# Three of seven row blocks of a depthwise convolution on TensorE, in the last pair of images

## The chip, the cores and the metric

The kernel runs on one core of one Trainium2 chip. The metric is the device time of one launch in microseconds. Below, VectorE, ScalarE, GpSimd (POOL) and TensorE (PE) are the four compute engines; SyncE (SP) issues most of the transfers. All data are fp32.

## What is computed

The reference has two layers over 32 images of 64 channels and 56 x 56 pixels. The first adds sums of products of two and of three channels of a group to its input. The second is an attention over the pixels with two softmaxes, and this change lies in what follows it:

```python
out = jnp.einsum('nabcd,nicd->niab', f, g)
out = out / h * w
out = jax.lax.conv_general_dilated(out, w_dw, (1, 1), ((1, 1), (1, 1)),
        dimension_numbers=('NCHW', 'OIHW', 'NCHW'), feature_group_count=n_in)
out = _bn(out, gamma2, beta2, mean2, var2)
return out + l
```

`feature_group_count=n_in` makes it a depthwise convolution: each channel has its own 3 x 3 filter, with one pixel of zeros around the image. `l` is the input of the second layer. The batch norm is a factor and an offset per channel; the kernel folds the factor into the nine weights (`wdt`, line 299) and keeps the offset as `bias2`.

## The kernel before

The images are worked in 16 pairs (`NP`), with 2 x 64 channels on the 128 partitions. A pair has 49 tiles of 128 query pixels (`IT`), and the main loop (line 889) takes one tile an iteration: two halves of scores on TensorE, negated and reduced by VectorE, two exponentials on ScalarE, and three iterations later (`LAG`) the product with the values, summed in PSUM over all tiles of an image. Work of the neighbouring pairs is put beside it. `put` (line 679) gives each piece a place, an iteration and a slot in it ("loads", "feed", "gap0", "gap1"); `pin` (line 89) then fixes the order of every engine to the order in which the program was written out. So each engine and each queue runs its list front to back.

After the last tile of an image, `take` divides the sums (`num`), `turn` transposes them (`tr`), and `place` (line 632) writes them by eight transfers an image into `tt`, a tile of 128 channels by 3136 pixels that all pairs share. The transfers go by halves of the image: pixels 0 to 1599 first (`j` = 0), the rest after.

The convolution reads `tt` and adds into `ys[n % 3]`, a tile in SBUF that holds `l`, one of three that rotate. The rows of the image are in five blocks (`NB`, `BLK`, line 309), of 11 rows, the last of 12. For each block, `conv_begin` (line 651) lets POOL add `bias2`; nine calls of `conv_step` (line 655) let VectorE add one tap each, `y = tt shifted * weight + y`, without the row or column that would lie outside the image; then `store` (line 671) starts the transfer to the output. The 45 steps of a pair are spread over the next pair's iterations (line 869 on). For the last pair nothing follows, and its steps come one after another behind the last tile.

The tiles that the change uses: `xs`, a tag of the pool `xp` with 13 buffers (line 315), holds loaded inputs of the first layer's products, the last of which belong to the last pair and are read by POOL one pair earlier; `ps`, four banks of PSUM, holds the scores.

Of the kernel before, what the change touches and what calls it, by code (L numbers as in the profile page):

```python
# [9 lines left out]
FP = mybir.dt.float32  # L10
AF = mybir.ActivationFunctionType
ALU = mybir.AluOpType
# [6 lines left out]
H = W = 56  # L19
# [3 lines left out]
HALF = NCH // 2  # L23
# [3 lines left out]
BANK = 512  # L27
# [8 lines left out]
PCH = -(-N // NPC)  # L36
# [33 lines left out]
def tile_poly_conv_attention(  # L70
# [12 lines left out]
    NP = B // 2  # L83
    IT = 2 * NQ + 1
# [29 lines left out]
    pe, dve, act, pool, sync = map(Pinned, (nc.tensor, nc.vector, nc.scalar, nc.gpsimd, nc.sync))  # L114

    const = ctx.enter_context(tc.tile_pool(name="const", bufs=1))
    xp = ctx.enter_context(tc.tile_pool(name="xp", bufs=2))
# [6 lines left out]
    ps = ctx.enter_context(tc.tile_pool(name="ps", bufs=1, space=PSUM))  # L124
# [7 lines left out]
    at = 0  # L132
    for s, (_, bs) in enumerate(STEPS):
        for h in range(2) if s < NSLOT else ():
            act.dma_start(
                out=wq[s::NSLOT, :, h, :],
                in_=wpoly[h * 32 : h * 32 + 32, at : at + NRND, h * 32 : h * 32 + 32],
# [5 lines left out]
    wdt = const.tile([128, 9], FP, name="wdt")  # L143
# [12 lines left out]
    for k in range(2):  # L156
        pe.matmul(
            out=ax[:, k * 256 : k * 256 + 256],
            lhsT=w4,
            rhs=wq.rearrange("p k h o -> p (k h o)")[:, :256],  # L160
            start=(k == 0),
            stop=True,
            skip_group_check=True,
        )
    dve.memset(ax, 0.0)
    tt = const.tile([128, N], FP, name="tt")
# [31 lines left out]
    ys = [yt[:, p, :] for p in range(3)]  # L198
# [68 lines left out]
    for k in range(NRND):  # L267
        by = row("beta2_0") if k == 0 else b3row
        w = wq[:, k, :, :].rearrange("p h o -> p (h o)")
        dve.tensor_tensor(w, w, by, ALU.mult)  # L270
    for half in (0, C):
        w = w4[:, half : half + C]
# [4 lines left out]
    t0 = const.tile([128, 1], FP, name="t0")  # L277
# [22 lines left out]
    bias2 = const.tile([128, 1], FP, name="bias2")  # L300
# [5 lines left out]

    prods = {}
    NB = 5
    BLK = [(b * H // NB, (b + 1) * H // NB) for b in range(NB)]
    stored = set()  # L310


# [2 lines left out]
    XB = {"x0": 7, "xs": 13, "xc": 3}  # L315
# [6 lines left out]
    def start(out, in_):  # L322
        credit[0] -= 1
        sync.dma_start(out=out, in_=in_)
# [193 lines left out]
    def tile_at(t):  # L518
        n, r = divmod(t, IT)
        return n, (0 if r < NQ else 2 if r == NQ else 1), r % (NQ + 1)  # L520
# [128 lines left out]
    TAPS = [(4, 1, 1)] + [(k, *divmod(k, 3)) for k in range(9) if k != 4]  # L649

    def conv_begin(n, b):
        blk = ys[n % 3][:, BLK[b][0] * W : BLK[b][1] * W]
        pool.tensor_scalar(blk, blk, bias2, None, ALU.add)

    def conv_step(n, i):
        b, i = divmod(i, 9)
        k, dy, dx = TAPS[i]
        r0, r1 = max(BLK[b][0], 1 - dy), min(BLK[b][1], H + 1 - dy)
        x0, x1 = max(0, 1 - dx), min(W, W + 1 - dx)
        yr = ys[n % 3].rearrange("p (r w) -> p r w", w=W)[:, r0:r1, x0:x1]  # L660
        tr = tt.rearrange("p (r w) -> p r w", w=W)
        dve.scalar_tensor_tensor(
            yr,
            tr[:, r0 + dy - 1 : r1 + dy - 1, x0 + dx - 1 : x1 + dx - 1],
            wdt[:, k : k + 1],
            yr,
            ALU.mult,
            ALU.add,
        )

    def store(n, b):
        stored.add((n, b))
        blk = slice(BLK[b][0] * W, BLK[b][1] * W)
        start(out[2 * n : 2 * n + 2].rearrange("b c n -> (b c) n")[:, blk], ys[n % 3][:, blk])


# [2 lines left out]
    def put(t, at, what):  # L679
        beside.setdefault((t, at), []).append(what)  # L680
# [5 lines left out]
    LAG = 3  # L686
# [54 lines left out]
    def ready(qs):  # L741

        end = min(N, (qs[-1] + 1) * QT)
        return next(c for c, (p, w) in enumerate(PCS) if p + w >= end)
# [59 lines left out]
    for n in range(NP):  # L804
        base = n * IT
# [7 lines left out]
        if n == 0:  # L813
# [3 lines left out]
            for c in range(NPC):  # L817
                todo += rounds(1, c, ALL, 2)
                if c >= NPC // 2 + 1:
                    k = min(2 if c < NPC - 1 else len(ga), sum(ready(g[2]) <= c for g in ga))  # L820
# [3 lines left out]
            at = [2 * base + free[i * (len(free) - 1) // (len(todo) - 1)] for i in range(len(todo))]  # L824
        elif n + 1 == NP:
            todo = gb
            at = [2 * (base + LAG) + 3 + 4 * i for i in range(len(gb))]
        else:
            at = []
# [30 lines left out]
        for b, end in ((2 * n, base + NQ), (2 * n + 1, base + IT - 1)):  # L860
            t = end + LAG
# [7 lines left out]
    for n in range(NP):  # L869
        t0 = n * IT + IT + LAG + 5  # L870
        more = range(2 * t0, 2 * ((n + 2) * IT - 1))
        if n + 1 < NP:
            more = [h for h in more if h // 2 != (n + 1) * IT + NQ + LAG]
            more = [h for h in more if h not in leaves] if len(more) - len(leaves & set(more)) >= 9 * NB else more
        for i in range(9 * NB):
            at = more[i * (len(more) - 1) // (9 * NB - 1)] if n + 1 < NP else 2 * t0 + i
            put(at // 2, f"gap{at % 2}", lambda n=n, i=i: conv_step(n, i))
            if i % 9 == 0:
                put(at // 2 - 2, "gap0", lambda n=n, b=i // 9: conv_begin(n, b))
            if i % 9 == 8:  # L880
                put(at // 2 + 1, "loads", lambda n=n, b=i // 9: store(n, b))
# [6 lines left out]
    t = 0  # L888
    while t < last + LAG or beside:
# [3 lines left out]
        if old:  # L893
            n, kind, q = tile_at(u)
# [111 lines left out]
```

## Time and profile before

| | us |
|---|---|
| three runs | 4959.59, 4962.83, 4973.32 |
| median of the runs | 4962.83 |
| the profiled execution | 4963.24 |
| its span, first to last instruction | 4961.4 |

| engine | busy, us | share of the span | instructions |
|---|---|---|---|
| PE, matmuls | 4711.5 | 95% | 118068 |
| ScalarE | 4554.6 | 92% | 2356 |
| VectorE | 4136.2 | 83% | 6106 |
| PE, weight loads | 3211.9 | 65% | 118068 |
| POOL | 3212.2 | 65% | 4325 |

The profile records one execution. Its page gives the busy time of each engine, the chain of waits that ended last, and groups of like instructions with their mean duration and with what ended the idle time before them. Its timeline gives start and length of instructions, its windows the busy time of each engine in a stretch, with the clock that TensorE was granted (PEclk, 1.00 is full speed). An average over the span says little about a single stage: the shares above are those of the steady loop, while the change lies in the last tens of microseconds and in preparations before them. All instructions of the main function carry the line of the helper that records them (108), so groups are told apart by the names of their tiles: `y<-tt,wdt,y` is a step of the convolution, `tt<-tr` a transfer of `place`, `out_dram<-y` a store.

### The profile page before, as it was taken

The page shows a single profiled execution, that of the slowest core. Times are in us where ns is not written, and L with a number is a line of the kernel's source. Part 1 is how long each engine was busy: PE and PEld are TensorE (multiplying, and loading weights), DVE is VectorE, ACT ScalarE, POOL GpSimd, SP SyncE. Part 2 cuts the span into 40 slices and gives each one's busy share as a digit, 9 for nine tenths or more (in the row PEclk, how much of TensorE's full clock was granted, in tenths as well). Part 3 has the DMA queues.
Part 4 walks back from the last instruction along what each step waited for, and adds up shares of the span by engine and source line. Part 5 has one row for each costly group of instructions (what it writes and reads, how often), then busy time and mean ns, then how long its engine had stood idle before and what let it go on. Part 6 is the DMA issues. An engine that isn't in the chain of part 4 may idle for free.

```text
span 4961.4 us, 263901 instructions
## 1 busy us (share of the span) xinstructions
PE 4711.5 (95%) x118068; PEld 3211.9 (65%) x118068; DVE 4136.2 (83%) x6106; ACT 4554.6 (92%) x2356; POOL 3212.2 (65%) x4325
## 2 busy tenths in 40 slices
PE   6988999999999999999999999999999999999885
PEld 2555666666666666666666666666666666666663
DVE  6545898988888898898988888888888888888787
ACT  1767999999999999999999999999999999999995
POOL 2676685857758586785857678585876858587000
PEclk9999999999999999999999999999999999999997
DMA  7555656565565556556565555656555565654101
GB/s 203 148 154 150 147 143 154 144 149 143 146 148 147 139 150 149 139 143 150 146 146 148 147 142 144 145 152 145 144 150 144 145 145 146 153 142 117 39 8 33
DMA packets 884029, 685.64 MB, mean 138 GB/s; under 512 B 290892, under 2 KB 868428, under 8 KB 878796
## 3 DMA queue, kind: packets, MB, share of 16 engines
q1 hardware_dynamic: 874892, 659.46, 52.1%
q8 instruction: 923, 15.12, 1.3%
q10 hardware_dynamic: 8000, 9.30, 0.6%
q14 instruction: 214, 1.75, 0.1%
HBM read 565.65 MB, written 25.69 MB: 119 GB/s over the span
## 4 chain that ended last, share of the span: by engine, by line
PE 76%; DVE 12%; DMA 3%; issue 3%; ACT 3%; POOL 1%; SPq 1%; ACTq 0%; POOLq 0%; DVEq 0%
PE av L108 33%; PE ps L108 25%; PE ax L108 18%; DVE e L108 10%; ACT e L108 3%; DMA xc_None<-in_x_dram 2%; DVE y L108 1%; SPq L108 1%; POOL p L108 1%; DVE num L108 1%; DMA x<-in_x_dram 1%; DMA first<-in_x_dram 1%; POOL q L108 0%; DMA xa<-in_x_dram 0%; ACTq L108 0%
## 5 line engine op out<-in xcount | busy, mean ns | idle before, releaser
L108 PEld LDWEIGHTS av<-gq,e 128*64 128x64 f32 x64512 | 2015.8, 138 | 945.6 <-issue 938.6
L108 ACT ACTIVATE e<-e,nm 128x3136 f32<-128x3136 f32 x784 | 2283.6, 2913 | 279.9 <-DVE e L108 264.0
L108 POOL TENSOR_TENSOR p<-q,x 128x242 f32<-128x242 f32 (+1 forms) x2418 | 1820.2, 786 | 842.6 <-PE ax L108 834.8
L108 ACT ACTIVATE e<-e,rz 128x3136 f32<-128x3136 f32 x784 | 2270.5, 2896 | 0.0
L108 PE MATMUL av<-gq,e 128*64 128x65 f32 x64512 | 2229.3, 225 | 4.3 <-ACT e L108 3.0
L108 DVE TENSOR_SCALAR_CACHE_REDUCE e<-ps 128x1568 f32<-128x1568 f32 x784 | 1403.4, 1790 | 312.7 <-PE ps L108 295.4
L108 DVE TENSOR_SCALAR_CACHE_REDUCE e<-ps,nm 128x1568 f32<-128x1568 f32 x784 | 1448.3, 1847 | 256.9 <-PE ps L108 251.4
L108 PE MATMUL ps<-th 32*64 32x392 f32 x25088 | 1450.2, 515 | 120.6 <-DVE e L108 110.8
L108 DVE SCALAR_TENSOR_TENSOR y<-tt,wdt,y 128x605 f32<-128x605 f32 (+4 forms) x720 | 726.2, 1009 | 6.7 <-DMA tt<-tr 5.2
L108 POOL TENSOR_TENSOR p<-q,xb 128x242 f32<-128x242 f32 x806 | 574.9, 740 | 218.8 <-PE ax L108 208.5
L108 POOL TENSOR_TENSOR q<-x,xa 128x242 f32<-128x242 f32 x806 | 570.9, 732 | 204.9 <-DMA xa<-in_x_dram 195.5
L108 PEld LDWEIGHTS ps<-th 32*64 32x64 f32 x25088 | 369.9, 130 | 463.1 <-DVE e L108 381.6
L108 PE MATMUL ax<-gq,e 128*64 128x65 f32 x12288 | 490.3, 222 | 1.2 <-issue 1.2
L108 PE MATMUL ax<-p,wq 128*32 128x242 f32 (+1 forms) x6448 | 477.8, 374 | 2.4 <-POOL p L108 1.4
L108 PEld LDWEIGHTS ax<-gq,e 128*64 128x64 f32 x12288 | 425.4, 138 | 1.5 <-issue 1.5
L108 PEld LDWEIGHTS ax<-p,wq 128*32 128x32 f32 x6448 | 178.4, 109 | 108.4 <-POOL p L108 15.7
L108 POOL TENSOR_SCALAR y<-y,bias 128x616 f32<-128x616 f32 (+1 forms) x80 | 149.1, 1864 | 149.2 <-PE ax L108 149.2
L108 DVE SCALAR_TENSOR_TENSOR y<-ax,bias,xc_None 128x242 f32<-128x242 f32 (+3 forms) x208 | 97.1, 467 | 120.7 <-PE ax L108 115.1
L108 POOL TENSOR_TENSOR p<-xc_None 128x242 f32<-128x242 f32 (+3 forms) x208 | 127.6, 614 | 105.2 <-DMA xc_None<-in_x_dram 85.3
L108 PE MATMUL ax<-p,w 128*32 128x242 f32 (+1 forms) x1612 | 125.1, 373 | 33.2 <-POOL p L108 33.2
L108 PE MATMUL ax<-wit,y 128*64 128x64 f32 x3136 | 143.8, 223 | 10.2 <-issue 6.1
L108 ACT ACTIVATION_READ_ACCUMULATOR e<-e,nm 128x1 f32 x784 | 145.7, 186 | 0.0
(80 smaller groups left out, 1348.9 us busy)
## 6 DMA issues: line engine op xcount, KB each, us to landing
x<-in_x_dram SPq DMA_DIRECT2D x2232, 121.0 KB
xa<-in_x_dram SPq DMA_DIRECT2D x744, 121.0 KB
xb<-in_x_dram SPq DMA_DIRECT2D x1488, 60.5 KB
th<-y SPq DMA_DIRECT2D x124, 392.0 KB
xc_None<-in_x_dram SPq DMA_DIRECT2D x360, 121.0 KB
x<-in_x_dram SPq DMA_DIRECT2D x186, 116.0 KB
out_dram<-y SPq DMA_DIRECT2D x64, 308.0 KB
tt<-tr SPq DMA_DIRECT2D x128, 100.0 KB
```

The lines of the kernel that those rows point to most:

```text
L108: i = f(*args, **kw)
```

## The change

Only the last pair (`n` = 15) is touched; `BLK` gets a list of blocks per pair, which is the old one for the first 15. The last pair has seven blocks of 8 rows. VectorE computes blocks 0 to 3 (rows 0 to 31, `NDVE` = 4) by nine steps each, as before. TensorE computes blocks 4 to 6 (rows 32 to 55): a depthwise tap is a product with a diagonal matrix of the tap's 128 weights, and nine such matmuls with shifted columns of `tt` are summed in one bank of PSUM a block. VectorE then adds this sum, `bias2` and `y` in one instruction a block, behind its own four blocks; POOL adds no bias to these three.

The nine diagonal matrices are made by POOL from an identity, in ten of the `xs` buffers, at the fourth iteration after the start of the last pair ("feed", iteration 739). All 27 matmuls are written out ahead of VectorE's 36 steps. Blocks 0 to 3 are stored after their steps and blocks 4 to 6 after their additions, so that the last pair has seven stores for five. In the lists of the engines, POOL's eleven new instructions stand ahead of the biases of the last pair but one.

```diff
-    BLK = [(b * H // NB, (b + 1) * H // NB) for b in range(NB)]
+    BLK = [[(b * H // NB, (b + 1) * H // NB) for b in range(NB)]] * (NP - 1)
+
+    BLK.append([(r, r + 8) for r in range(0, H, 8)])
+    NDVE = 4
...
+    def make_diags():
+
+        eye = xp.tile([128, PCH], FP, name="eye", tag="xs", bufs=XB["xs"])[:, :128]
+        pool.memset(eye, 0.0)
+        pool.affine_select(
+            out=eye, in_=eye, compare_op=ALU.not_equal, fill=1.0, base=0, pattern=[[-1, 128]],
+            channel_multiplier=1,
+        )
+        for k in range(9):
+            t = xp.tile([128, PCH], FP, name=f"diag_{k}", tag="xs", bufs=XB["xs"])[:, :128]
+            pool.tensor_scalar(t, eye, wdt[:, k : k + 1], None, ALU.mult)
+            diags.append(t)
+
+    def conv_matmuls(n, blocks):
+        acc = ps.tile([128, HALF, BANK], FP, name="conv", tag="ps")
+        tr = tt.rearrange("p (r w) -> p r w", w=W)
+        for j, b in enumerate(blocks):
+            for i in range(9):
+                k, dy, dx, r0, r1, x0, x1 = tap(n, b, i)
+                rb = BLK[n][b][0]
+                o = acc[:, j, : 8 * W].rearrange("p (r w) -> p r w", w=W)
+                pe.matmul(
+                    out=o[:, r0 - rb : r1 - rb, x0:x1],
+                    lhsT=diags[k],
+                    rhs=tr[:, r0 + dy - 1 : r1 + dy - 1, x0 + dx - 1 : x1 + dx - 1],
+                    start=(i == 0),
+                    stop=(i == 8),
+                    skip_group_check=True,
+                )
+        return {b: acc[:, j, : 8 * W] for j, b in enumerate(blocks)}
+
+    def conv_end(n):
+
+        blocks = range(NDVE, len(BLK[n]))
+        accs = conv_matmuls(n, blocks)
+        for b in range(NDVE):
+            for i in range(9):
+                conv_step(n, 9 * b + i)
+            store(n, b)
+        for m in blocks:
+            y = ys[n % 3][:, BLK[n][m][0] * W : BLK[n][m][1] * W]
+            dve.scalar_tensor_tensor(y, accs[m], bias2, y, ALU.add, ALU.add)
+            store(n, m)
...
+        if n + 1 == NP:
+            put(n * IT + LAG + 1, "feed", make_diags)
+            for b in range(NDVE):
+                put(t0 - 4, "gap0", lambda n=n, b=b: conv_begin(n, b))
+            put(t0, "gap0", lambda n=n: conv_end(n))
+            break
         for i in range(9 * NB):
-            at = more[i * (len(more) - 1) // (9 * NB - 1)] if n + 1 < NP else 2 * t0 + i
+            at = more[i * (len(more) - 1) // (9 * NB - 1)]
```

`tap`, which the diff takes out of `conv_step`, gives the weight's number, the shift and the rows and columns that a tap reaches. `conv_begin`, `conv_step` and `store` index `BLK` by the pair.

More of the change, by code (lines that the diff above doesn't have):

```diff
@@ L651, in conv_begin, with tap @@
     def conv_begin(n, b):
-        blk = ys[n % 3][:, BLK[b][0] * W : BLK[b][1] * W]
+        blk = ys[n % 3][:, BLK[n][b][0] * W : BLK[n][b][1] * W]
         pool.tensor_scalar(blk, blk, bias2, None, ALU.add)
+    def tap(n, b, i):
+        k, dy, dx = TAPS[i]
+        r0, r1 = max(BLK[n][b][0], 1 - dy), min(BLK[n][b][1], H + 1 - dy)
+        x0, x1 = max(0, 1 - dx), min(W, W + 1 - dx)
+        return k, dy, dx, r0, r1, x0, x1
     def conv_step(n, i):
         b, i = divmod(i, 9)
-        k, dy, dx = TAPS[i]
-        r0, r1 = max(BLK[b][0], 1 - dy), min(BLK[b][1], H + 1 - dy)
-        x0, x1 = max(0, 1 - dx), min(W, W + 1 - dx)
+        k, dy, dx, r0, r1, x0, x1 = tap(n, b, i)
         yr = ys[n % 3].rearrange("p (r w) -> p r w", w=W)[:, r0:r1, x0:x1]
@@ L669, in conv_step @@
         )
+    diags = []
+    def make_diags():
[14 more added lines that the diff above has]
+            for i in range(9):
+                k, dy, dx, r0, r1, x0, x1 = tap(n, b, i)
+                rb = BLK[n][b][0]
[20 more added lines that the diff above has]
+            store(n, m)
     def store(n, b):
         stored.add((n, b))
-        blk = slice(BLK[b][0] * W, BLK[b][1] * W)
+        blk = slice(BLK[n][b][0] * W, BLK[n][b][1] * W)
         start(out[2 * n : 2 * n + 2].rearrange("b c n -> (b c) n")[:, blk], ys[n % 3][:, blk])
```

## The prediction

> **What bounds the kernel now.** The summary says that the kernel is bound by VectorE, ScalarE and TensorE in turn, but the change touches one stage only, so I went from the page to the last stretch. The timeline of the last 70 us comes first (start, length, engine, operation):
>
> ```profile
> 4909.54 0.64 PE L108 MATMUL ax<-gq,e 128*64 128x65 f32 x16
> ...
> 4911.57 1.90 DVE L108 STREAM_TRANSPOSE tr<-num 128x800 f32<-128x800 f32 x2
> 4918.71 39.58 DVE L108 SCALAR_TENSOR_TENSOR y<-tt,wdt,y 128x616 f32<-128x616 f32 x45 [5.23 <-DMA tt<-tr]
> 4926.55 32.13 SPq L108 DMA_DIRECT2D out_dram<-y  x5
> ```
>
> TensorE's last matmul ends at 4910.2. VectorE waits until 4918.71 for the transfers into `tt`, then runs the 45 steps of the last pair's convolution alone until 4958.29. The fifth store follows, and the span ends at 4961.4, 3.1 us later. The chain of waits agrees: from 4918.71 on it holds nothing but these steps. So this stage is VectorE's alone, and a microsecond taken from it is a microsecond of the span. The groups of the same stretch give durations (busy us, mean ns):
>
> ```profile
> L108 DVE SCALAR_TENSOR_TENSOR y<-tt,wdt,y 128x605 f32<-128x605 f32 x24 | 20.4, 848 | 0.9
> L108 DVE SCALAR_TENSOR_TENSOR y<-tt,wdt,y 128x616 f32<-128x616 f32 x12 | 10.3, 858 | 5.5 <-DMA tt<-tr 5.2
> ...
> L108 DVE SCALAR_TENSOR_TENSOR y<-tt,wdt,y 128x672 f32<-128x672 f32 x2 | 1.8, 915 | 0.0
> ```
>
> From 616 to 672 elements the time grows by 57 ns, 1.02 ns an element; I use 1.04, which also fits the 550-element row (792 ns). Over the stage the 45 steps cover 27,556 elements per partition ((56+55+55) rows by (56+55+55) columns, since edge taps lose a row or a column). 27,556 x 1.0417 ns = 28.70 us, and the rest of 39.58 us is 10.88 us, or 0.242 us a step.
>
> **VectorE's part of the change.** Four blocks of 8 rows keep 36 steps and (31+32+32) x 166 = 15,770 elements: 16.43 + 36 x 0.242 = 25.1 us. Removed are 9 steps and 11,786 elements: 12.28 + 2.18 = 14.45 us. Added are three additions that read PSUM, 448 wide. A row of the first stage is nearly the same instruction (PSUM, a column and an SBUF tile in, SBUF out), though on 64 partitions:
>
> ```profile
> L108 DVE SCALAR_TENSOR_TENSOR y<-first_s,bias,first 64x448 f32<-64x448 f32 x4 | 2.7, 671 | 1.9 <-PE first_s L108 1.9
> ```
>
> With the 0.02 us between instructions that is 3 x 0.69 = 2.07 us. Net, if TensorE is in time: 14.45 - 2.07 = **12.4 us**. The removed part alone bounds the gain: it cannot pass 14.5 us even if the three additions were free.
>
> **TensorE's part.** 27 matmuls with 71 x 166 = 11,786 columns; in this trace each fp32 matmul appears as two records with a weight load each, so 54 passes. A pass of 448 columns takes 0.373 us: the weight loads of the first stage come as one pair per pass of two column groups at 32.16, 32.54, 32.91, and as one per 0.745 us (24.44, 25.18, 25.93) before the clock rose. That is 0.833 ns a column at full clock and 1.66 at half. All passes: 11,786 x 2 x 0.833 = 19.6 us at full clock.
>
> The clock will be low at first. TensorE has then idled for ten microseconds, and the last 42 us of the span show a granted clock of 0.50. How fast it rises shows at the last place where it fell (columns: window, its length, busy time and count of PE, PEld, DVE, ACT, POOL, then PEclk, DMA share, GB/s):
>
> ```profile
> 4903.50:4904.00 0.50, 0.50 (x24) 0.50 (x20) 0.00 (x0) 0.50 (x1) 0.00 (x0) 0.88 0.00 0
> 4904.00:4904.50 0.50, 0.50 (x14) 0.50 (x12) 0.00 (x0) 0.50 (x1) 0.00 (x0) 0.50 0.00 0
> ...
> 4907.00:4907.50 0.50, 0.50 (x18) 0.50 (x17) 0.00 (x0) 0.00 (x0) 0.00 (x0) 0.70 0.17 33
> 4907.50:4908.00 0.50, 0.50 (x24) 0.50 (x22) 0.00 (x0) 0.00 (x0) 0.00 (x0) 1.00 0.00 0
> ```
>
> It was low for 3.3 us, although TensorE was busy throughout. Elsewhere a burst after an idle stretch began at 42.2 and rose at 46.7; the burst of 23.7 rose near 30. I take 3.4 to 6.8 us of half clock, half of which is lost: 1.7 to 3.4, middle 2.6 us. With 0.2 us to fill and drain, the burst lasts 21.5 to 23.2, middle 22.4 us.
>
> It starts later than VectorE. The blocks of rows 32 to 55 need the second half of `tt`, whose last transfer is issued at 4917.41; the one VectorE waits for was issued at 4916.03 and landed 2.60 us later. The same 2.60 gives 4920.0, so TensorE starts at 4920.1 and ends at 4941.6 to 4943.3. VectorE's own 36 steps end at 4918.71 + 25.1 = 4943.8. The first addition waits for all 27 matmuls, and finds them ready with 0.5 to 2.2 us to spare. Behind that wait stand only the three additions and their stores. If the cover is gone, every microsecond of TensorE beyond 4943.8 is one of the span.
>
> **Rule against row: the weight loads.** The Trainium skill ("TensorE: Matmul & The Clock Gate", Part 3, The mechanism) says that a weight load overlaps a running matmul only when its row group differs. Here all 54 loads fill the whole array, so by this rule none is hidden, and each would add, by the same page's section on LDWEIGHTS, 128 / 1.2 = 107 ns: 5.8 us, an estimate. TensorE would end at 4948.3 and the gain would be 7.9 us. The only whole-array matmuls of the trace are the four records at the start:
>
> ```profile
> 9.83 1.35 PEld L108 LDWEIGHTS ax<-wq,w 128*128 128x128 f32 x4 [9.83 <-issue]
> 9.86 2.04 PE L108 MATMUL ax<-wq,w 128*128 128x256 f32 x4 [9.86 <-DMA rowt<-in_rows_dram]
> ```
>
> The second to fourth loads start at 9.99, 10.42 and 10.85. Their pitch of 0.43 us is the streaming of 256 columns at half speed (256 x 1.66 = 0.425), with the 0.33 us load inside it. So the row says hidden, and I follow it; these are the same row groups and the nearest row. By the same page's back-to-back formula, N/2.4 + 2.5 ns, a pass of 448 columns takes 0.19 us and the burst 10 us; the measured 0.373 decides.
>
> **POOL and SP.** POOL makes an identity (a memset, one select) and nine scaled copies of 128 x 128. The scaled bias rows (1839 ns at 616, 1964 at 672) give 2.2 ns an element, so 0.75 us a copy, 6.8 us for nine; the select has no row, between the memset's 0.2 us and a few us. They run before POOL's biases for the pair before last, at 4565.8, whose first use on VectorE is at 4659.07; POOL is then idle for 75 us. Eight to twelve us vanish in it. One bias fewer is run, in idle time too. SP issues 7 stores of 224 KB for 5. The last four follow VectorE at 0.69 us. A store of 336 KB moved at 409 GB/s for about 0.9 us at the end of the trace, so 224 KB need 0.6 us and do not queue; the smaller last one gains about 0.2 us.
>
> **Sum.** The profiled execution took 4963.24 us, its span 4961.4 with 1.8 around it; the median shown, 4962.83, is 0.4 below. Saved: 12.4 + 0.2 = 12.6 of the span: 4950.7 from the profile, 4950.2 from the median. I forecast **4950.5 us**.
>
> **Rivals.**
> 1. *The weight loads are exposed.* For it: the rule above. Against it: the start row, and weight loads that overlap matmuls all through the middle of the kernel, though there in two column groups. With 0.107 us a load: 4955; with half of the row's 0.333 at half clock, 0.167: 9.0 us more on TensorE, 4958.
> 2. *Slower: TensorE stays at half clock to the end.* Its burst then takes 39.2 + 0.2 us, ends at 4959.5, and the additions end at 4961.6, against 4958.29 before: 3.1 us slower, 4966. It decides from a burst of 36 us on (4958.3 - 2.1 - 4920.1). For it: the clock was 0.50 in the whole tail, and near 23.7 a burst stayed low for over 6 us. Against: every burst of the trace that lasted 7 us reached 1.00.
> 3. *The sum is right, but the measurement carries it past a bound.* The bound that a measurement of this kernel can tell from no change is about 0.3%, 14.9 us; 12.6 us is 2.3 us short of it, and three runs of the same kernel lie 13.7 us apart. The time is then 4944 to 4948.
> 4. *The change does not do what it says*, because the matmuls and the steps do not run side by side. They share only `tt`, which both read; no row speaks for it. The burst would follow the 36 steps: 4943.8 + 22.4 + 2.1 = 4968.3 against 4958.3, 10 us slower, 4973.
>
> **Chances.** Forecast, with the measured value within the bound: 0.50. Exposed loads: 0.10. Past the bound on the fast side: 0.33. Half clock to the end: 0.04. No overlap, or a cost that I have not seen: 0.03, and only this last is slower by over 0.3%. So faster by over 0.3%: 0.33; within 0.3%: 0.64; slower: 0.03. The range, 4945 to 4958 us, reaches from the scatter on the fast side to exposed loads on the slow side.
>
> **What would show it.** In the profile of the changed kernel: 36 steps of about 0.70 us and three of 0.67 from PSUM at the end; TensorE's burst starting a microsecond after VectorE's first step, its pitch falling from 0.75 to 0.37 us within 7 us, and its end before VectorE's 36th step, so that the first addition shows no idle time; the clock column at 0.50 and then 1.00; the ten `diag` instructions on POOL near 4566 with nobody waiting. Idle time of VectorE before the first addition, released by TensorE, would put the error in the burst: a pitch above 0.37 at clock 1.00 means exposed loads, a clock of 0.50 throughout the second rival. Anything above 14.5 us saved would have to come from outside this stage.

## The result, and the profile after

The changed kernel takes 4947.44 us (median of 6 runs, 4945.21 to 4950.35) against 4964.29 us (6 runs, 4959.59 to 4973.32): a ratio of 0.9965 with a 95% interval of 0.9952 to 0.9978. The forecast was 4950.5 us, the range 4945 to 4958. The profiled execution took 4948.12 us with a span of 4946.3, 15.1 us less than before.

The timeline of its last stretch answers to the one shown of before (start, length, engine, operation):

```profile
4907.11 0.64 PE L108 MATMUL ax<-gq,e 128*64 128x65 f32 x16
...
4909.15 1.91 DVE L108 STREAM_TRANSPOSE tr<-num 128x800 f32<-128x800 f32 x2
4916.27 25.16 DVE L108 SCALAR_TENSOR_TENSOR y<-tt,wdt,y 128x448 f32<-128x448 f32 x36 [5.22 <-DMA tt<-tr]
...
4917.77 21.71 PE L108 MATMUL conv<-tt,diag 128*128 128x448 f32 x54 [10.02 <-DMA tt<-tr]
...
4922.56 21.01 SPq L108 DMA_DIRECT2D out_dram<-y  x7
...
4941.35 1.86 DVE L108 SCALAR_TENSOR_TENSOR y<-conv,bias,y 128x448 f32<-128x448 f32 x3
```

TensorE's burst lies wholly beside VectorE's 36 steps: it begins 1.50 us after the first of them and ends at 4939.48, 1.9 us before the first addition. The addition has no bracket behind it, so it waited for nobody.

Below, **the stage** is the time from VectorE's first step of the last pair to the end of the span. It was 4961.4 - 4918.71 = 42.69 us and is 4946.3 - 4916.27 = 30.03 us: 12.66 us less. The other 2.4 us of the two profiles lie ahead of the stage, where the kernels differ only in POOL's preparations. (The page gives a span to 0.1 us, so a stage read in this way is good to about 0.05 us.)

The groups of the stretch, which answer to those of before (busy us, mean ns | idle time before):

```profile
L108 DVE SCALAR_TENSOR_TENSOR y<-tt,wdt,y 128x440 f32<-128x440 f32 x22 | 14.9, 677 | 0.8
...
L108 PEld LDWEIGHTS conv<-tt,diag 128*128 128x128 f32 x54 | 11.0, 205 | 20.3 <-issue 19.7
...
L108 DVE SCALAR_TENSOR_TENSOR y<-tt,wdt,y 128x448 f32<-128x448 f32 x11 | 7.5, 683 | 5.5 <-DMA tt<-tr 5.2
...
L108 DVE SCALAR_TENSOR_TENSOR y<-conv,bias,y 128x448 f32<-128x448 f32 x3 | 1.9, 677 | 0.0
```

A step of 448 elements takes 683 ns where one of 616 took 858: a quarter fewer elements save only a fifth of the time, since a part of each step is fixed. The 54 weight loads are busy for 11.0 us, half of the burst. The loads in the timeline, and the windows with the granted clock (the number before the DMA share; the columns are those of the windows in the prediction), show whether that time is added to the matmuls:

```profile
4919.39 0.34 PEld L108 LDWEIGHTS conv<-tt,diag 128*128 128x128 f32 x1 [0.41 <-issue]
4920.12 0.34 PEld L108 LDWEIGHTS conv<-tt,diag 128*128 128x128 f32 x1 [0.40 <-issue]
...
4921.78 0.19 PEld L108 LDWEIGHTS conv<-tt,diag 128*128 128x128 f32 x1 [0.19 <-issue]
4922.15 0.19 PEld L108 LDWEIGHTS conv<-tt,diag 128*128 128x128 f32 x1 [0.18 <-issue]
...
4937.36 1.50 PEld L108 LDWEIGHTS conv<-tt,diag 128*128 128x128 f32 x5 [0.18 <-issue]
```

```profile
4920.00:4921.00 1.00, 1.00 (x3) 0.48 (x2) 0.96 (x2) 0.00 (x0) 0.00 (x0) 0.50 0.00 0
4921.00:4922.00 1.00, 1.00 (x4) 0.57 (x3) 0.93 (x3) 0.00 (x0) 0.00 (x0) 0.90 0.00 0
4922.00:4923.00 1.00, 1.00 (x4) 0.49 (x3) 1.00 (x2) 0.00 (x0) 0.00 (x0) 1.00 0.00 0
```

The loads come every 0.73 us at a clock of 0.50 and every 0.37 us at 1.00. Is that pitch the time in which the columns of a pass stream through, or is a part of it the load? The passes at the end of the burst answer it. They lose a row of the image and have 385 or 392 columns instead of 440 or 448. The five last loads span 1.50 us, so four passes take 1.50 - 0.19 = 1.31 us, 0.33 us each: the pitch falls in proportion to the columns, while the load is the same. So the pitch is the streaming time alone, and a load of 0.19 us within it adds nothing. The clock was low from 4917.77 to about 4921.2, 3.4 us of the burst.

POOL's preparations in the timeline stand where they were expected, at 4565. They take 6.3 us, and no wait for them shows in the profile:

```profile
4564.87 0.21 POOL L108 MEMSET eye<- 128x128 f32 x1
4565.15 0.29 POOL L108 TENSOR_SCALAR_AFFINE_SELECT eye<-eye 128x128 f32<-128x128 f32 x1
4565.54 5.59 POOL L108 TENSOR_SCALAR diag<-eye,wdt 128x128 f32<-128x128 f32 x9
```

### The profile page after: what moved, and what is told of

Its sections match the earlier page's. It is cut to its first block, busy times and chain, and to the rows that moved or that the text cites. A ratio compares the mean times of both kernels' runs of the same rounds, so it can differ in the third digit from the quotient of the medians.

```text
span 4946.3 us, 264020 instructions
## 1 busy us (share of the span) xinstructions
PE 4734.2 (96%) x118122; PEld 3218.8 (65%) x118122; DVE 4125.5 (83%) x6100; ACT 4554.4 (92%) x2356; POOL 3222.6 (65%) x4335
## 4 chain that ended last, share of the span: by engine, by line
PE 77%; DVE 12%; DMA 3%; issue 3%; ACT 3%; POOL 1%; SPq 1%; ACTq 0%; DVEq 0%; POOLq 0%
PE av L108 33%; PE ps L108 26%; PE ax L108 18%; DVE e L108 10%; ACT e L108 3%; DMA xc_None<-in_x_dram 1%; POOL p L108 1%; DVE y L108 1%; DMA first<-in_x_dram 1%; DVE num L108 1%; DMA x<-in_x_dram 1%; SPq L108 1%; DMA xa<-in_x_dram 0%; DVE rd L108 0%; ACTq L108 0%
## 5 line engine op out<-in xcount | busy, mean ns | idle before, releaser
L108 DVE SCALAR_TENSOR_TENSOR y<-tt,wdt,y 128x605 f32<-128x605 f32 (+6 forms) x711 | 713.1, 1003 | 6.4 <-DMA tt<-tr 5.2
L108 POOL TENSOR_SCALAR y<-y,bias 128x616 f32<-128x616 f32 (+2 forms) x79 | 146.9, 1860 | 98.9 <-PE ax L108 98.9
```

The costliest lines, as they stand in the source:

```text
L108: i = f(*args, **kw)
```

## The experiments

Two things were open. The medians differ by 16.9 us and the stage by 12.7: does the change also shorten what comes before the stage? And is it true that VectorE alone sets the end, so that TensorE's burst, its clock and its weight loads are free? Every row of this table is one kernel on the chip; "stage" is read from its profile, the ratio is to the kernel before in the same rounds.

| kernel | stage expected, us | stage, us | median, us (runs) | ratio, 95% interval |
|---|---|---|---|---|
| before | | 42.69 | 4964.29 (6) | |
| changed | | 30.03 | 4947.44 (6) | 0.9965, 0.9952 to 0.9978 |
| changed, again | 30.0 | 30.06 | 4949.87 (12) | 0.9975, 0.9967 to 0.9984 |
| seven blocks on VectorE | 46.9 | 46.97 | 4967.67 (12) | 1.0009, 1.0001 to 1.0017 |
| clock kept up | 30.0 | 30.11 | 4950.96 (20) | 0.9979, 0.9973 to 0.9986 |
| three blocks on VectorE, four on TensorE | 35.7 | 35.9 | 4955.95 (20) | 0.9988, 0.9981 to 0.9994 |
| two large blocks on VectorE | 28.0 | 28.18 | 4948.07 (15) | 0.9973, 0.9965 to 0.9980 |
| five blocks on VectorE, two on TensorE | 35.7 | 35.8 | 4956.63 (12) | 0.9995, 0.9987 to 1.0004 |
| two blocks, all on VectorE | 37.2 | 37.47 | 4956.78 (12) | 0.9991, 0.9983 to 0.9999 |
| two blocks, early addition, clock kept up | 25.6 to 26.3 | 26.01 | 4945.03 (6) | 0.9969, 0.9957 to 0.9980 |
| changed, beside the next | 30.0 | 30.11 | 4949.53 (9) | 0.9974, 0.9962 to 0.9986 |
| two blocks, early addition, clock kept up, beside the one above | 26.0 | 25.98 | 4945.40 (6) | 0.9962, 0.9948 to 0.9977 |

**The change again**, unaltered.

> The changed kernel once more, unaltered, in five rounds beside the kernel before. What is open is why the median fell by 16.9 us where the last stage alone, read from VectorE's first step of the last pair to the end of the span, went from 42.7 to 30.0 us, 12.7 us less. Theory A (the change saves only in the last stage, the rest is scatter of what comes before it): the stage is again 30.0 us within 0.3, the start of the stage lies anywhere between 4915 and 4921 us, and the ratio is nearer to 0.9974 (12.7 us). Rival B (the change also shortens what comes before, by some 4 us, through the shorter biases on POOL): the start of the stage is again near 4916 and the ratio is again near 0.9965.

The stage is 30.06 us, its start 4917.74, the ratio 0.9975: 12.4 us. That is theory A's number. The first ratio lies a few microseconds on the fast side of it, and the two intervals overlap. The kernel before had medians of 4962.35 (57 runs), 4961.60 (37) and 4962.70 us (15) in the rounds of the later rows. Taking its stage from each median of this table leaves 4918.9 to 4920.9 us for what comes ahead, for all kernels and rounds but those of the first comparison, which leaves 4921.6 us before and 4917.4 after. So the 4.2 us that the first comparison has above the stage are scatter on both of its sides, and no kernel shows them again.

**TensorE's share taken back.**

```diff
-    NDVE = 4
+    NDVE = 7
-        accs = conv_matmuls(n, blocks)
+        accs = conv_matmuls(n, blocks) if blocks else {}
```

> Seven blocks of 8 rows, all on VectorE, with the diagonal matrices made and not used: the change without TensorE's share. Theory A: 63 steps over the same 27,556 elements, 28.7 + 63 x 0.242 = 43.9 us of VectorE and 3.0 to the end, so a stage of 46.9 us and a time some 4.2 us above the kernel before. Rival B (what comes before the stage is shortened by the work put on POOL and the shorter biases): the same time as before or less, since 4 us are won ahead of the stage.

The timeline has the 63 steps, in 43.93 us where 43.9 were computed:

```profile
4919.03 43.93 DVE L108 SCALAR_TENSOR_TENSOR y<-tt,wdt,y 128x448 f32<-128x448 f32 x63 [5.23 <-DMA tt<-tr]
```

The kernel is slower than before by the ratio and by its stage (46.97 us). POOL's work ahead of the stage is as in the changed kernel, apart from three more short biases, and it wins nothing: rival B has fallen. The starts of the stage say the same. In the ten profiles without a long stall (see the last section) they lie between 4915.00 and 4920.39 us, and the kernel before, with 4918.71 in the one profile of it, is in their midst.

**TensorE's clock kept up** by twelve matmuls whose sums nobody reads.

```diff
         acc = ps.tile([128, HALF, BANK], FP, name="conv", tag="ps")
+        for _ in range(12):
+            pe.matmul(
+                out=acc[:, 3, : 8 * W], lhsT=diags[0], rhs=ys[(n - 1) % 3][:, : 8 * W],
+                start=True, stop=True, skip_group_check=True,
+            )
```

> Twelve matmuls that nobody reads are put on TensorE between its last attention matmul and the wait for tt, so that its clock does not fall. Theory A (TensorE's burst is hidden behind VectorE's 36 steps, with 2 us to spare): the burst shrinks from 21.7 to about 19.9 us and ends some 3.8 us ahead of the first addition, and the stage stays at 30.0 us. Rival C (the additions wait for TensorE): the stage falls by 1.8 us to 28.2.

The twelve take 9.29 us of the time in which TensorE was idle, and the granted clock is 1.00 from 4920 to the end of the burst. The burst is 20.02 us instead of 21.71, as expected, and the additions follow the 36 steps as in the changed kernel:

```profile
4928.79 25.16 DVE L108 SCALAR_TENSOR_TENSOR y<-tt,wdt,y 128x448 f32<-128x448 f32 x36 [5.22 <-DMA tt<-tr]
...
4930.02 20.02 PE L108 MATMUL conv<-tt,diag 128*128 128x448 f32 x54 [0.53 <-DMA tt<-tr]
...
4953.87 1.86 DVE L108 SCALAR_TENSOR_TENSOR y<-conv,bias,y 128x448 f32<-128x448 f32 x3
```

The stage does not move (30.11 us). A burst 1.7 us shorter is worth nothing while VectorE ends last: rival C has fallen.

**Another split.** `NDVE = 3` gives TensorE four blocks, `NDVE = 5` two.

> Four of the seven blocks on TensorE, three on VectorE. Theory A: VectorE's 27 steps take 12.3 + 6.5 = 18.8 us; TensorE's 36 matmuls take 26.3 us at full clock and about 28.7 with the slow start, begin 1.5 us after VectorE and end at 30.2; the four additions wait for all of them and add 2.6: 32.8, and 2.9 to the end, a stage of 35.7 us with about 11 us of VectorE idle before the first addition. Rival D (the weight loads slow a longer burst, or both engines slow each other): longer than 37 us. Rival E (the first three additions run before the last matmuls end): 33.8.

> Five of the seven blocks on VectorE, two on TensorE. Theory A: VectorE bounds: 45 steps over 19,754 elements, 20.6 + 10.9 = 31.5 us, two additions of 0.65, 2.9 to the end: a stage of 35.7 us, with no idle time before the additions. Any rival in which TensorE or the additions' wait set the end of the changed kernel: less than 33 us.

With four blocks on TensorE the timeline shows the wait that the changed kernel just avoids:

```profile
4915.00 18.85 DVE L108 SCALAR_TENSOR_TENSOR y<-tt,wdt,y 128x448 f32<-128x448 f32 x27 [5.21 <-DMA tt<-tr]
...
4916.55 28.73 PE L108 MATMUL conv<-tt,diag 128*128 128x448 f32 x72 [10.07 <-DMA tt<-tr]
...
4945.32 2.46 DVE L108 SCALAR_TENSOR_TENSOR y<-conv,bias,y 128x448 f32<-128x448 f32 x4 [11.47 <-PE conv L108]
```

VectorE is done at 4933.85 and idles for 11.47 us until TensorE's burst of 28.73 us (28.7 computed) ends. Rivals D and E have fallen with it. With two blocks on TensorE it is the other way round: the burst takes 16.36 us and VectorE 31.48, without idle time before the additions:

```profile
4919.00 31.48 DVE L108 SCALAR_TENSOR_TENSOR y<-tt,wdt,y 128x448 f32<-128x448 f32 x45 [5.21 <-DMA tt<-tr]
4920.51 16.36 PE L108 MATMUL conv<-tt,diag 128*128 128x448 f32 x36 [10.02 <-DMA tt<-tr]
...
4950.39 1.27 DVE L108 SCALAR_TENSOR_TENSOR y<-conv,bias,y 128x448 f32<-128x448 f32 x2
```

Both splits cost 5.8 to 5.9 us of stage. TensorE set the end with four blocks and was free with three; the wait of the additions for all matmuls, which was marked in the prediction, is real. (The ratio of the second split, 0.9995, is nearer to 1 than the 0.9986 that its stage would give, by a little more than its interval; two of its 12 runs were long, 4965.57 and 4974.39 us.)

**Fewer, larger steps on VectorE.**

```diff
-    BLK.append([(r, r + 8) for r in range(0, H, 8)])
-    NDVE = 4
+    BLK.append([(0, 16), (16, 32), (32, 40), (40, 48), (48, 56)])
+    NDVE = 2
```

> VectorE's 32 rows in two blocks of 16 instead of four of 8; TensorE's part as in the changed kernel. Theory A: VectorE loses 18 steps, 18 x 0.242 = 4.4 us, and is done after 20.8 us; TensorE's burst ends 23.2 us after VectorE's first step (0.9 more or less by the clock), so now the additions wait for it for about 2.4 us; they take 1.9, and 2.9 go to the end: a stage of 28.0 us against 30.0. Rival (a step costs only its elements): a stage of 30 us.

```profile
4926.42 20.84 DVE L108 SCALAR_TENSOR_TENSOR y<-tt,wdt,y 128x896 f32<-128x896 f32 x18 [5.22 <-DMA tt<-tr]
...
4949.95 1.87 DVE L108 SCALAR_TENSOR_TENSOR y<-conv,bias,y 128x448 f32<-128x448 f32 x3 [2.69 <-PE conv L108]
```

VectorE saves 4.3 us, and the additions now wait 2.69 us for TensorE, so that the stage gains 1.85. This is the slack of 1.9 us seen from the other side: 4.3 - 1.9 leaves a wait of 2.4, and the burst was 0.28 us longer in this profile (21.99 us). A step costs more than its elements.

**The last pair wholly on VectorE, in two blocks of 28 rows**, with no diagonal matrices:

```diff
+    BLK.append([(0, 28), (28, 56)])
+    NDVE = 2
...
-            put(n * IT + LAG + 1, "feed", make_diags)
```

> The last pair wholly on VectorE in two blocks of 28 rows, without diagonal matrices or TensorE. Theory A: 18 steps, 28.7 + 18 x 0.242 = 33.1 us, and a last store of 784 KB that takes 2.0 us to move instead of 0.6: 4.1 to the end, a stage of 37.2 us, 5.5 below the kernel before and 7.2 above the changed one. Rival (a step costs only its elements): 42 us.

```profile
4918.93 33.12 DVE L108 SCALAR_TENSOR_TENSOR y<-tt,wdt,y 128x1568 f32<-128x1568 f32 x18 [5.23 <-DMA tt<-tr]
```

The 18 steps take 33.12 us (33.1 computed), the stage 37.47. So 5.2 of the 12.7 us could be had on VectorE alone, by fewer steps, without TensorE.

**All of it together**: two blocks on VectorE, one PSUM tile a block, the first addition between VectorE's two blocks, and the twelve idle matmuls.

```diff
+    BLK.append([(0, 16), (16, 32), (32, 40), (40, 48), (48, 56)])
+    NDVE = 2
...
+        accs = [pa.tile([128, BANK], FP, name=f"conv_{j}", tag=f"av{j}") for j in range(NK)]
+        for _ in range(12):
...
+        order = [0, 2, 1, 3, 4]
+        for b in order:
+            if b < NDVE:
+                for i in range(9):
+                    conv_step(n, 9 * b + i)
+            else:
+                y = ys[n % 3][:, BLK[n][b][0] * W : BLK[n][b][1] * W]
+                dve.scalar_tensor_tensor(y, accs[b], bias2, y, ALU.add, ALU.add)
+            store(n, b)
```

> Two blocks of 16 rows on VectorE, three of 8 on TensorE in three tiles of PSUM of their own, each addition as soon as its block is due (after VectorE's first block, and two at the end), and twelve idle matmuls that keep the clock up. Theory A: VectorE needs 20.8 + 1.9 = 22.7 us, TensorE ends 21.5 us after VectorE's first step, the last stores queue a little: a stage of 25.6 to 26.3 us, 4 us below the changed kernel. Rival C (TensorE's burst or its clock does not matter to the end): no difference to the kernel with two blocks, 28.0.

```profile
4919.89 10.38 DVE L108 SCALAR_TENSOR_TENSOR y<-tt,wdt,y 128x896 f32<-128x896 f32 x9 [5.24 <-DMA tt<-tr]
...
4930.19 0.68 DVE L108 SCALAR_TENSOR_TENSOR y<-conv,bias,y 128x448 f32<-128x448 f32 x1
...
4930.78 10.54 DVE L108 SCALAR_TENSOR_TENSOR y<-tt,wdt,y 128x896 f32<-128x896 f32 x9
4941.24 1.27 DVE L108 SCALAR_TENSOR_TENSOR y<-conv,bias,y 128x448 f32<-128x448 f32 x2
```

The stage is 26.01 us; VectorE runs from 4919.89 to 4942.51 with no idle time before any addition, beside a burst of 20.02 us. Medians of the same kernel differ by a few microseconds from one set of rounds to the next, so this version was run once more beside the changed kernel.

> The changed kernel unaltered, on the same chip and in the same rounds as the kernel of the next run. Theory A: a stage of 30.0 us and a ratio within 0.9965 to 0.9985, as in the first repetition (0.9975). Rival B (the change also shortens what comes before the stage, by some 4 us): 0.9965 or less.

> The kernel with two blocks on VectorE, separate PSUM tiles, early addition and idle matmuls, beside the changed kernel. Theory A: the stage is 4.0 us shorter (26.0 against 30.0), and the medians of the two differ by 4 us within the scatter of 2 us. If the medians do not differ, what the stage saves is lost where the stage's own profile does not show it.

The stages are 30.11 and 25.98 us, the medians 4949.53 and 4945.40: 4.1 us by both. This version beats both kernels. It was not tried how much of the step from 28.18 us the idle matmuls alone bring, and how much the early addition; by the sums, TensorE without the idle matmuls would end 1.7 us later and then be last.

## Why the prediction was right

**The sum.** Forecast were 12.4 us from VectorE and 0.2 from the last store, 12.6 in all; the stage fell by 12.66 and, in two later profiles of the same code, by 12.63 and 12.58. By terms: the 36 steps were computed at 25.1 us and took 25.08 from first start to first addition. The three additions were put at 2.07 and took 1.86, since the records of neighbours overlap a little when none has to wait. The end behind VectorE was expected to shrink by 0.2 and did not; it is 3.1 us in both profiles. Here the prediction was wrong: it had the stores not queue, but the four last ones run into each other. The DMA columns of the windows show them moving without a gap from 4942.3 to 4944.8 at 337 to 387 GB/s, where the single store of before had 403 (4959.3 to 4959.8). That the sum came out is in this part luck: two errors of 0.2 us cancelled. POOL's preparations were oversized as well, at eight to twelve us instead of 6.3 (a copy of the identity takes 0.62 us, not 0.75), which costs nothing.

**TensorE's burst.** Start 1.4 us after VectorE: 1.50. Length 21.5 to 23.2 us: 21.71, with 22.04, 21.99 and 21.50 in other profiles of the same burst. The clock rises sooner or later in it: 3.0 us after its start in the one of 21.50 us, 4.1 us in the one of 22.04. Spare time before the first addition 0.5 to 2.2 us: 1.9. The three runs with another split or other steps moved the wait to where this slack says.

**Rule against row.** The Trainium skill's rule ("TensorE: Matmul & The Clock Gate", Part 3, The mechanism), that a weight load overlaps a running matmul only when its row group differs, would have cost an estimated 5.8 us with the page's time for a load, and 10.3 us with the 0.19 us of this trace. The trace contradicts it for these whole-array loads, by 0.19 us of load within a pitch of 0.37 and by a pitch that follows the columns down to 0.33. The prediction used half of what that section says. The same section also lets a load run ahead of running matmuls when it targets the background weight buffer. The trace agrees with that half, though no run shows the buffer itself. The row of four records at the start of the kernel was enough to see that the loads are hidden.

**The rivals.** Exposed loads, half clock to the end and lack of overlap show in no profile. The third, a right sum whose measurement lies past the bound, is what the first comparison gave: 0.35% and 4947.44 us, within the 4944 to 4948 us named for it, and the chance for it was put at 0.33. Two repetitions gave 0.25% and 0.26%, on the near side. The surplus comes from the stretch ahead of the stage, whose end differs by 4.1 us between three profiles of the same changed kernel (4916.27, 4917.74 and 4920.39 us). What moves that stretch by a few microseconds from one execution to the next was not traced.

## What to carry to other kernels

Where a stage is a chain of steps on one engine, split its time into a part per element and a fixed part per step before moving work away: here 10.9 of 39.6 us were fixed, and larger steps alone returned 5.2 us. When work goes to a second engine, compute both ends, with the later start and the low clock of the second, and place the cut where they meet; one block to either side cost 5.8 us. A gain of a quarter of a percent is read from the stage in the trace, where it repeats within 0.1 us (30.03, 30.06 and 30.11), and not from medians that scatter by several.

## What the runs showed of the hardware

Two profiles began the stage late, at 4926.42 (two large blocks) and 4928.79 (clock kept up), 8.1 and 10.5 us behind the mean of the ten others. In both, one step of the convolution of an earlier pair took 7.37 and 6.16 us instead of 0.85; no other such step took more than 2.5 us in any of the twelve profiles. The timeline of the second, with POOL's rows of the same time:

```profile
1240.96 4.70 POOL L108 TENSOR_TENSOR p<-q,x 128x242 f32<-128x242 f32 x7
1245.63 1.99 POOL L108 TENSOR_TENSOR p<-q,xb 128x242 f32<-128x242 f32 x3
```

```profile
1242.11 6.16 DVE L108 SCALAR_TENSOR_TENSOR y<-tt,wdt,y 128x605 f32<-128x605 f32 x1
```

POOL runs ten products back to back until 1247.62, and VectorE's step, which reads two tiles of SBUF, ends 0.65 us later. In the other profile POOL's chain ends at 3001.84 and the step at 3002.51. That is not the rule of the kernel: at the same place of the kernel before, the same step took 0.87 us in the midst of a chain of fifteen products on POOL, and the product beside it took 1.25 us, where its neighbours took 0.70:

```profile
1242.91 1.25 POOL L108 TENSOR_TENSOR p<-q,x 128x242 f32<-128x242 f32 x1
```

```profile
1242.71 0.87 DVE L108 SCALAR_TENSOR_TENSOR y<-tt,wdt,y 128x605 f32<-128x605 f32 x1
```

The Trainium skill ("SBUF — State Buffer", SBUF: two separate sides) says that a VectorE operation with two SBUF inputs and a POOL operation that reads SBUF exclude each other for a whole instruction, whichever starts first. Both views agree with that: in the kernel before the product seems to wait for the step, and in the stalled executions the step for the products. But there it waited through eight of POOL's instructions in a row, and not through one. No experiment here takes POOL's chain away, so the cause is argued from these rows and not shown. The stall has a consequence on TensorE. It idles for 4.79 us, and its clock falls to 0.50:

```profile
1250.09 1.61 PE L108 MATMUL ps<-th 32*64 32x392 f32 x16 [4.79 <-DVE e L108]
```

```profile
1250.00:1260.00 10.00, 9.91 (x154) 7.36 (x156) 6.98 (x16) 5.80 (x3) 0.00 (x0) 0.50 0.69 197
```

The clock stays at 0.50 until about 1268, although TensorE is busy for 9.91 us of the ten shown. How the 10.5 us divide between the stall and the low clock was not traced. Why VectorE mostly gets in between two products, and in these two executions did not, stays open. A stall of this kind may lie behind the single long runs of each kernel, but no such run of the unchanged kernel was profiled.
